# Shifting activation slots and weight tiles within SBUF, without touching an instruction

## The chip, the core and the metric

The kernel runs on one core of a Trainium2 chip. The metric is the device time of one execution in microseconds (us), as the median of several runs. A lower number is better.

## The reference, cut to what matters

The input `x` has shape (4, 1024, 256) in fp32. Three residual layers follow each other. The first and the third are the same gated feed-forward network with ternary weights, the second is a long convolution (a state-space kernel evaluated through an FFT) with a projection.

```python
x = x + 0.5 * ffn(layernorm(x))
x = x + (gelu(causal_conv(layernorm(x), K)) @ W.T + b)
x = x + 0.5 * ffn(layernorm(x))

def ffn(x):                                     # widths 256 -> 1024 -> 1024 -> 1024 -> 256
    h = silu((x @ w1.T) * s1) * ((x @ w2.T) * s2)
    h = gelu((h @ h1.T) * t1)
    h = gelu((h @ h2.T) * t2)
    return (h @ w3.T) * s3
```

Nearly all of the arithmetic is in the two feed-forward layers, and most of that in the two 1024 x 1024 products with `h1` and `h2`.

## The kernel before, in words

The 4096 rows of `x` are cut into 8 blocks of 512 rows (`TB = 512`). Each block goes through the feed-forward network once for the first layer (tiles with `_f` in their names) and once for the third (`_g`), so there are 16 passes of `ffn`. All five weight matrices stay in SBUF for the whole kernel, in the pool `keep`, as the tiles `w1_sb`, `w2_sb` (8 KB per partition each), `h1_sb`, `h2_sb` (32 KB each) and `w3_sb` (8 KB). The profile cuts digits and buffer numbers out of the names, so `w1_sb`, `w2_sb` and `w3_sb` are all `w_sb` there, and `h1_sb` and `h2_sb` are both `h_sb`.

Weights are ternary, so they are exact in the fp32r format. Activations are held as two fp32r parts, a rounded one and the remainder (`parts = 2`), and every product is done twice, once for each part, into the same PSUM bank. A tile of activations is therefore 128 partitions by 2 by 512 numbers, 4096 bytes per partition. These tiles (`xt`, `ha`, `h2`, `h3`) share one set of 15 slots, given out by the helper `ring` (line 134), one slot directly after the other in SBUF. Tiles of 512 numbers (`half`, 2048 bytes) share another set of 19 slots.

The inner work is `linear` (line 235): for every output tile of 128 features it goes over the input tiles `k` and the two parts, and issues one matmul each:

```python
for k in range(n):
    for part in range(parts):
        nc.tensor.matmul(ps, w[:, k, m * P : (m + 1) * P], acts[k][:, part, :], ...)
```

The first operand is the stationary one: a block of 128 columns of a weight tile, 512 bytes per partition. The second is the moving one: 512 numbers of one part, 2048 bytes per partition. In a trace each such call is a LDWEIGHTS (engine row PEld) and a MATMUL (row PE). The LDWEIGHTS of the next call runs while the MATMUL of the present one streams. In the last product (line 295, tiles `po`) the roles are swapped: 128 columns of an activation slot are stationary and 256 columns of `w3_sb` are moving.

One pass of `ffn` issues 64 matmuls into `pa` and `pb` (the products with `w1` and `w2`), 256 into `p` (with `h1` and `h2`) and 64 into `po`. Sixteen passes make 5120 matmuls of 512 moving columns and 1024 of 256 moving columns, all in fp32r. The rest of TensorE's matmuls are in fp32: transposes of the normalised input (`pt`, line 225), the taps of the convolution's kernel (`pk`, line 497), and the transforms and projection of the middle layer (`pf` line 561, `pi` line 731, `pw` line 751).

ScalarE applies the activation out of PSUM (lines 258 and 271) and writes the rounded part (lines 261 and 273). VectorE multiplies by the gate (line 259) and forms the remainder (line 217). The convolution's own work is woven in by generators that are advanced once per output tile. A tile framework inserts the semaphores and orders each engine's instructions.

Where tiles lie: the allocator places each pool's tiles one after another. Before the change `w1_sb` starts at byte 17,408 of each partition, `w2_sb` at 25,600, `h1_sb` at 33,792, `h2_sb` at 66,560 and `w3_sb` at 99,328, and the ring's slots start at 165,376 and then every 4096 bytes (from 169,472, with small tiles in between, once more shifted by a multiple of 512). Every one of these numbers is a multiple of 512, and so is the offset of every column block inside a weight tile and of every part inside a slot.

Of the kernel before, what the change touches and what calls it, by code (L numbers as in the profile page):

```python
# [17 lines left out]
P = 128  # L18
B, L, D = 4, 1024, 256
HID = 1024  # L20
J = L // P
DC = D // P
KH = HID // P
# [68 lines left out]
def macaron_layers(  # L92
# [25 lines left out]
    wide = F32R if split else F32  # L118
    parts = 2 if split else 1
    keep = ctx.enter_context(tc.tile_pool(name="keep", bufs=1))  # L120
    work = ctx.enter_context(tc.tile_pool(name="work", bufs=2))
# [11 lines left out]

    def ring(name, *shape, dtype=F32):

        return work.tile([P, *shape], dtype, tag="ring", name=name, bufs=15)

    sc_sb = keep.tile([P, 4, KH], F32, name="sc_sb")  # L140
    cst_sb = keep.tile([P, CST_WIDTH], F32, name="cst_sb")
    ident = keep.tile([P, P], F32, name="ident")
    make_identity(nc, ident)
    w1_sb = keep.tile([P, DC, HID], wide, name="w1_sb")
    w2_sb = keep.tile([P, DC, HID], wide, name="w2_sb")
    h1_sb = keep.tile([P, KH, HID], wide, name="h1_sb")
    h2_sb = keep.tile([P, KH, HID], wide, name="h2_sb")
    w3_sb = keep.tile([P, KH, D], wide, name="w3_sb")
    wt_sb = keep.tile([P, DC, D], F32, name="wt_sb")
    w3s_sb = keep.tile([P, D], F32, name="w3s_sb")  # L150
    bias_sb = keep.tile([P, D], F32, name="bias_sb")
# [67 lines left out]
    def transposed(xn, name):  # L219

        xt = []
        for k in range(DC):
            pt = bank(f"pt_{name}_{k}")
            for i in range(JT):
                nc.tensor.transpose(  # L225
                    pt[:, i * P : (i + 1) * P], xn[:, i, k * P : (k + 1) * P], ident
                )
            t = ring(f"xt_{name}_{k}", parts, TB, dtype=wide)
            nc.vector.tensor_copy(t[:, 0, :], pt)  # L229
            if split:  # L230
                low_part(t, pt)
            xt.append(t)
        return xt
# [13 lines left out]
    def ffn(xt, src, dst, blk, name, tick, ahead):  # L247
# [4 lines left out]
        for m in range(KH):  # L252
            pa, pb = bank(f"pa_{name}_{m}"), bank(f"pb_{name}_{m}")
            linear(pa, w1_sb, m, xt)
            linear(pb, w2_sb, m, xt)
            g = half(f"g_{name}_{m}")
            t = ring(f"ha_{name}_{m}", parts, TB, dtype=wide)
            nc.scalar.activation(g, pa, AF.Silu, scale=sc_sb[:, 0, m : m + 1])  # L258
            stt(g if split else t[:, 0, :], pb, sc_sb[:, 1, m : m + 1], g, ALU.mult, ALU.mult)  # L259
            if split:  # L260
                nc.scalar.copy(t[:, 0, :], g)  # L261
                low_part(t, g)
            ha.append(t)
        for layer, w in ((2, h1_sb), (3, h2_sb)):
            hb = []
            for m in range(KH):
                ps = bank(f"p{layer}_{name}_{m}")
                linear(ps, w, m, ha)
                t = ring(f"h{layer}_{name}_{m}", parts, TB, dtype=wide)
                g = half(f"g{layer}_{name}_{m}") if split else t[:, 0, :]  # L270
                nc.scalar.activation(g, ps, AF.Gelu, scale=sc_sb[:, layer, m : m + 1])  # L271
                if split:
                    nc.scalar.copy(t[:, 0, :], g)  # L273
                    low_part(t, g)
                hb.append(t)
                if layer == 3:
                    ahead()
                if m < KH - 1:
                    tick()
            ha = hb  # L280
# [558 lines left out]
def macaron_kernel(tc: tile.TileContext, *args):  # L839
    nc = tc.nc  # L840
    with tc.tile_pool(name="flag", bufs=1) as flags:
        bad = flags.tile([1, 1], I32, name="bad")
        macaron_layers(tc, bad, *args)
        n_bad = nc.values_load(bad, min_val=0, max_val=1 << 24)
        with tc.If(n_bad > 0):
            macaron_layers(tc, None, *args)
# [65 lines left out]
```

## Time and profile before

| what | value |
|---|---|
| median of 3 runs | 1465.45 us (1464.86 to 1466.04) |
| the profiled execution, its own time | 1466.05 us |
| its span, first to last instruction | 1464.1 us |
| time outside the span | 1.95 us |
| mean granted TensorE clock | 0.995 |
| TensorE matmul busy | 1429.7 us, 98% |
| VectorE / ScalarE / GpSimd busy | 59% / 45% / 5% |

The span is the time from the first to the last instruction. A matmul's recorded duration contains its latency, which overlaps the next matmul; the pace of a stream is therefore read from how many matmuls start in a stretch of time, not from the duration of one.

### The profile page before, as it was taken

How to read it: one execution, taken by the hardware profiler on the slowest of the kernel's cores; microseconds unless marked ns; L12 is line 12 of the kernel's file. 1: busy time of each engine (PE TensorE's matmuls, PEld its weight loads, DVE VectorE, ACT ScalarE, POOL GpSimd, SP SyncE). 2: the span in 40 equal slices, each digit the busy share in tenths (PEclk: the TensorE clock that was granted, in tenths of full speed). 3: DMA queues.
4: the chain of work that ended last, by engine and by line, in shares of the span. 5: the costliest groups of instructions: out<-in, count | busy, mean ns of one | idle time of the engine just before them, and what ended most of it. 6: DMA issues, size and time to landing. Idle time of an engine off the chain costs nothing.

```text
span 1464.1 us, 18076 instructions
## 1 busy us (share of the span) xinstructions
PE 1429.7 (98%) x7074; PEld 1213.7 (83%) x7074; DVE 860.5 (59%) x1616; ACT 666.1 (45%) x996; POOL 74.4 (5%) x71
## 2 busy tenths in 40 slices
PE   5999999999999999997999999999999999999997
PEld 4788888888888888886888888888888888888886
DVE  5776574765744634667367673676736667464521
ACT  3677353783534434442454344543445334353432
POOL 2000000000000000000100001000010000100000
PEclk9999999999999999999999999999999999999999
DMA  9110000100001111210312113121121111633000
GB/s 365 33 42 2 15 30 4 40 1 29 15 29 44 62 46 38 72 58 29 101 51 87 37 36 94 48 89 37 36 94 44 65 37 36 221 117 101 21 9 17
DMA packets 42975, 85.50 MB, mean 58 GB/s; under 512 B 4737, under 2 KB 9985, under 8 KB 42881
## 3 DMA queue, kind: packets, MB, share of 16 engines
q1 hardware_dynamic: 39088, 72.73, 15.1%
q0 software_dynamic: 3792, 11.54, 2.2%
q8 instruction: 57, 0.93, 0.3%
q14 instruction: 38, 0.30, 0.1%
HBM read 69.05 MB, written 15.20 MB: 58 GB/s over the span
## 4 chain that ended last, share of the span: by engine, by line
PE 94%; DMA 2%; DVE 2%; ACT 1%; issue 0%; POOL 0%; SPq 0%; POOLq 0%; DVEq 0%
PE p_f L239 32%; PE p_g L239 30%; PE po_f L295 4%; PE po_g L295 4%; PE pa_g L239 4%; PE pb_g L239 4%; PE pa_f L239 3%; PE pb_f L239 3%; PE pi L731 2%; PE pf_m L561 2%; PE pk L497 2%; PE pw L751 2%; DMA x_f<-in_x_dram 1%; DMA k_in<-in_kin_dram 1%; PE pt_f L225 1%; DVE given L328 1%
## 5 line engine op out<-in xcount | busy, mean ns | idle before, releaser
L239 PE MATMUL p_f<-ha_f,h_sb 128*128 128x512 f32 x1024 | 242.4, 394 | 1.8 <-ACT ha_f L261 0.9
L239 PE MATMUL p_f<-h_f,h_sb 128*128 128x512 f32 x1024 | 240.4, 392 | 0.0
L239 PE MATMUL p_g<-h_g,h_sb 128*128 128x512 f32 x1024 | 236.0, 390 | 0.0
L239 PE MATMUL p_g<-ha_g,h_sb 128*128 128x512 f32 x1024 | 234.5, 390 | 0.0
L239 PEld LDWEIGHTS p_f<-ha_f,h_sb 128*128 128x128 f32 x1024 | 192.2, 189 | 43.5 <-ACT ha_f L261 1.6
L239 PEld LDWEIGHTS p_g<-ha_g,h_sb 128*128 128x128 f32 x1024 | 192.2, 188 | 39.9
L239 PEld LDWEIGHTS p_g<-h_g,h_sb 128*128 128x128 f32 x1024 | 192.2, 188 | 39.8
L239 PEld LDWEIGHTS p_f<-h_f,h_sb 128*128 128x128 f32 x1024 | 190.9, 188 | 40.0 <-DVE h_f L217 0.3
L271 ACT ACTIVATE g_g<-p_g,sc_sb 128x512 f32<-128x512 f32 x128 | 88.2, 689 | 273.4 <-PE p_g L239 268.6
L217 DVE TENSOR_TENSOR h_f<-g_f,h_f 128x512 fp32r<-128x512 f32 x128 | 88.3, 691 | 193.0 <-ACT h_f L273 192.8
L271 ACT ACTIVATE g_f<-p_f,sc_sb 128x512 f32<-128x512 f32 x128 | 88.0, 688 | 245.6 <-PE p_f L239 245.3
L217 DVE TENSOR_TENSOR h_g<-g_g,h_g 128x512 fp32r<-128x512 f32 x128 | 88.4, 691 | 171.4 <-ACT h_g L273 171.1
L273 ACT CAST h_g<-g_g 128x512 fp32r<-128x512 f32 x128 | 79.4, 620 | 3.9
L273 ACT CAST h_f<-g_f 128x512 fp32r<-128x512 f32 x128 | 79.1, 619 | 3.4
L258 ACT ACTIVATE g_g<-pa_g,sc_sb 128x512 f32<-128x512 f32 x64 | 44.0, 687 | 66.5 <-PE pa_g L239 64.4
L239 PE MATMUL pa_f<-xt_f,w_sb 128*128 128x512 f32 x256 | 70.5, 395 | 1.8 <-DVE xt_f L229 1.2
L259 DVE SCALAR_TENSOR_TENSOR g_g<-pb_g,sc_sb,g_g 128x512 f32<-128x512 f32 x64 | 47.9, 748 | 37.2 <-PE pb_g L239 29.8
L239 PE MATMUL pb_f<-xt_f,w_sb 128*128 128x512 f32 x256 | 69.2, 392 | 0.0
L239 PE MATMUL pa_g<-xt_g,w_sb 128*128 128x512 f32 x256 | 68.6, 390 | 0.0
L239 PE MATMUL pb_g<-xt_g,w_sb 128*128 128x512 f32 x256 | 68.4, 389 | 0.0
L295 PE MATMUL po_g<-w_sb,h_g 128*128 128x256 f32 x512 | 64.2, 285 | 2.2 <-DVE h_g L217 2.2
L295 PEld LDWEIGHTS po_g<-w_sb,h_g 128*128 128x128 f32 x512 | 62.3, 192 | 2.9 <-DVE h_g L217 2.8
(216 smaller groups left out, 1682.3 us busy)
## 6 DMA issues: line engine op xcount, KB each, us to landing
h_sb<-in_h_dram POOLq DMA_DIRECT2D x8, 1024.0 KB, 22.6
given<-in_h_dram SPq DMA_DIRECT2D x32, 256.0 KB, 4.7
kr<-k_hat SPq DMA_DIRECT2D x20, 256.0 KB, 2.7
ki<-k_hat SPq DMA_DIRECT2D x20, 256.0 KB, 2.9
x_f<-in_x_dram SPq DMA_DIRECT2D x8, 512.0 KB, 3.8
xr_f<-in_x_dram SPq DMA_DIRECT2D x16, 256.0 KB, 3.5
x<-y_f SPq DMA_DIRECT2D x16, 256.0 KB, 2.4
xm<-x SPq DMA_DIRECT2D x8, 512.0 KB, 4.1
```

The lines of the kernel that those rows point to most:

```text
L217: tt(t[:, 1, :], src, t[:, 0, :].bitcast(F32), ALU.subtract)
L225: nc.tensor.transpose(pt[:, i * P : (i + 1) * P], xn[:, i, k * P : (k + 1) * P], ident)
L239: nc.tensor.matmul(ps, w[:, k, m * P : (m + 1) * P], acts[k][:, part, :], start=(k == 0 and part == 0), stop=(k == n - 1 and part == parts ...
L258: nc.scalar.activation(g, pa, AF.Silu, scale=sc_sb[:, 0, m : m + 1])
L259: stt(g if split else t[:, 0, :], pb, sc_sb[:, 1, m : m + 1], g, ALU.mult, ALU.mult)
L271: nc.scalar.activation(g, ps, AF.Gelu, scale=sc_sb[:, layer, m : m + 1])
L273: nc.scalar.copy(t[:, 0, :], g)
L295: nc.tensor.matmul(ps[:, e * D : (e + 1) * D], ha[k][:, part, (i + e) * P : (i + e + 1) * P], w3_sb[:, k, :], start=(k == 0 and part == 0) ...
L497: nc.tensor.matmul(pk[:, at + i, :, :].rearrange("p h b -> p (h b)"), a[:, i].rearrange("p a b -> p (a b)"), qd[d1 // per_tile][:, at + i, ...
L561: nc.tensor.matmul(ps[e][:, part, :], m[:, e, part, :], rows_of(q + JQ * e), start=True, stop=True)
L731: nc.tensor.matmul(banks[dc][e][:, q * P : (q + 1) * P], vs[q + JQ * e][:, part, dc * P : (dc + 1) * P], m[:, e, part, :], start=(part == ...
L751: nc.tensor.matmul(ps[:, e * D : (e + 1) * D], yts[dc][j // JQ][:, (j % JQ + e) * P : (j % JQ + e + 1) * P], wt_sb[:, dc, :], start=(dc == 0),
```

## The change

The change moves tiles in SBUF and does nothing else. A ring slot becomes 8 numbers (32 bytes) longer than the tile it holds, so that neighbouring slots start 4128 bytes apart. Each of the five weight tiles gets a gap of 8 to 112 numbers behind it. The tile handed to the rest of the kernel is a view with the same shape as before. The gaps add up to 1024 bytes, so the tiles that follow the weights keep their places modulo 512.

```diff
     def ring(name, *shape, dtype=F32):
-        return work.tile([P, *shape], dtype, tag="ring", name=name, bufs=15)
+        a, b = shape
+        t = work.tile([P, a * b + 8], dtype, tag="ring", name=name, bufs=15)
+        return t[:, 0 : a * b].rearrange("p (a b) -> p a b", a=a)
+
+    def spaced(name, k, width, gap):
+        t = keep.tile([P, k * width + gap], wide, name=name)
+        return t[:, 0 : k * width].rearrange("p (k o) -> p k o", k=k)
...
-    w1_sb = keep.tile([P, DC, HID], wide, name="w1_sb")
-    w2_sb = keep.tile([P, DC, HID], wide, name="w2_sb")
-    h1_sb = keep.tile([P, KH, HID], wide, name="h1_sb")
-    h2_sb = keep.tile([P, KH, HID], wide, name="h2_sb")
-    w3_sb = keep.tile([P, KH, D], wide, name="w3_sb")
+    w1_sb = spaced("w1_sb", DC, HID, 8)
+    w2_sb = spaced("w2_sb", DC, HID, 24)
+    h1_sb = spaced("h1_sb", KH, HID, 112)
+    h2_sb = spaced("h2_sb", KH, HID, 24)
+    w3_sb = spaced("w3_sb", KH, D, 88)
```

In the built program the start addresses become, modulo 512: `w1_sb` 0, `w2_sb` 32, `h1_sb` 128, `h2_sb` 64, `w3_sb` 160, and the 15 slots 0, 32, 64 and so on to 448. The instructions of every engine are the same, in the same order and with the same shapes.

## The prediction

> **What bounds the kernel now.** I read the first part of the page, then the waits of TensorE, then the chain of waits in order of time.
>
> ```profile
> PE 1429.7 (98%) x7074; PEld 1213.7 (83%) x7074; DVE 860.5 (59%) x1616; ACT 666.1 (45%) x996; POOL 74.4 (5%) x71
> PEclk9999999999999999999999999999999999999999
> PE 94%; DMA 2%; DVE 2%; ACT 1%; issue 0%; POOL 0%; SPq 0%; POOLq 0%; DVEq 0%
> ```
>
> TensorE is busy for 98% of the span, its clock is never throttled, and the chain that ended last runs through it for 94%. The waits confirm that nobody holds it up for long; these rows are "who waited, for whom: us in total, times, longest":
>
> ```profile
> PE pt_f L225 <- DVE x_f L211: 13.8, 1, 13.8
> PE pi L731 <- DVE v_False L722: 7.4, 1, 7.4
> PE po_g L295 <- DVE h_g L217: 2.2, 2, 1.3
> ```
>
> One wait at the start, one in the middle layer, and 2 us for the activations. So the end is set by the pace of the matmul stream itself. The chain in order of time gives that pace; its rows are start, length, then what and how many:
>
> ```profile
> 767.59 54.42 PE p_g L239 x240
> 822.88 7.67 PE po_g L295 x64
> 884.87 6.91 PE pw L751 x32
> ...
> 208.38 3.63 PE p_f L239 x16
> 212.01 0.80 PE pk L497 x8
> 212.81 3.78 PE p_f L239 x16
> ```
>
> Dividing: an fp32r matmul of 512 moving columns takes 54.42/240 = 226.75 ns, one of 256 columns 7.67/64 = 119.84 ns. The difference, 106.9 ns for 256 columns, is 0.4176 ns a column, so 512 columns stream in 213.8 ns and **12.9 ns per matmul do not depend on the columns**. The third row is fp32: 6.91/32 = 215.9 ns for 256 columns, at half the rate[...]. So each of the 6144 fp32r matmuls seems to carry some 10 ns that a fp32 one doesn't. All of them have both operands starting at a multiple of 512 bytes, and in the trace the LDWEIGHTS for the next matmul starts 3 or 4 ns after the present matmul.
>
> The last three rows are a second clue. Sixteen matmuls take 3.63 us when the stream is settled (226.9 ns each), but 3.78 us after eight small `pk` matmuls. The single starts after such a break lie 324, 235, 233, 236, 224, 231, 236, 228, 233, 230 and then 227 ns apart: the first is a weight load that nothing covered, and about nine more run slow until the two streams are in step again. The pace thus depends on how the weight stream and the moving stream lie against each other in time. That is what an address could act on.
>
> [...]
>
> **The change part by part.**
>
> *Instructions.* None is added, removed or moved, on any engine or queue; no wait is added. In the before version all 6078 pairs of a streaming fp32r matmul and the next fp32r weight load start at distance 0 modulo 512. Counted from the new addresses, the distances spread over all sixteen multiples of 32, between 277 and 428 pairs each; 397 stay at 0.
>
> *TensorE, the term that decides.* The trace has no fp32r matmul at another distance, so I bound it. The best case removes the whole 10.4 ns: 6144 x 10.4 = 63.9 us. The worst is priced among the rivals. For the value between I use the speeds. The `pk` rows, 0.80/8 = 100 ns each with only 16 columns to stream, are paced by weight loads, so a load walks its 512 bytes in about 100 ns. The moving stream walks 512 bytes (128 columns) in 128 x 0.4176 = 53 ns. During one load it makes about two rounds modulo 512 while the weights make one. Started together they meet at the beginning and once more one round later, at the end; started apart they meet once, in the middle. If a meeting is what costs, **half the excess goes**: 32 us, for 15 in 16 of the pairs: 30.0 us. That is a reading of the clues, not something that the trace shows.
>
> *VectorE and ScalarE* read and write the same slots in the same order. They have 41% and 55% of the span free, and TensorE waits for them 2 us at a time at most once the stream has begun, the middle layer's 7.4 us apart, which touches no ring tile. Their reads and writes already sweep through all places modulo 512. I price them at nothing. What hides them is TensorE's own stream; faster matmuls thin that cover, and `ha` and `h` (lines 261 and 217) would be late first, at layer boundaries. Bounds: 1 us gained, 3 us lost over the 32 layer boundaries and the 16 `po`.
>
> *DMA.* The weights land in rows shifted by multiples of 32 bytes. The first matmul waits for `x_f` (the 13.8 us), and the first stretch of 50 us has 17 us of idle TensorE, in which weight loads of 9.0 and 22.6 us play a part. Bytes and packets are the same, so nothing; bounds plus or minus 1 us.
>
> *Sum.* Against the profiled execution, which took 1466.05 us (span 1464.1 and 1.95 around it): 1466.05 - 30.0 = 1436.0. The median of the runs is 0.6 us lower, 1465.45; against it 1435.5, my forecast.
>
> **The rivals.**
>
> *A fixed cost of fp32r (no change, 1465.4).* The 12.9 ns may be the price of swapping fp32r weights, whatever the addresses. For it: it is 226.75 to the ns in settled stretches, equal for 512 and 256 columns, whatever VectorE and ScalarE do meanwhile[...]. Against it: after a break single distances fall to 224 and rise to 236, which a fixed cost doesn't explain.
>
> *The streams no longer settle (slower, 1479).* Today every operand starts at the same place, so after some nine matmuls the two streams find a step in which 226.75 ns repeat. Of 3.78 - 3.63 = 0.15 us lost after a break about 0.10 us is the uncovered load (324 - 227 ns), and 0.05 us is spread over nine matmuls: 5.5 ns each. With slots 32 bytes apart, the moving operand changes its place in 2491 of 5053 consecutive pairs of 512-column matmuls (the two parts of one slot keep it). If each such change is a new disturbance of 5.5 ns, 13.7 us are lost: 1479. If the stream never settles, all 6144 pay: 33.8 us, 1499. This decides when the disturbance outweighs what the distance gives, by more than 0.5 ns a matmul.
>
> *The full removal (1402).* Only distance 0 and its neighbours cost anything, all others run at 216 ns. For it speaks only that the fp32 rows show such a floor.
>
> *The change doesn't do what it says.* The places of the five weight tiles hardly matter: 15 slots at 15 of 16 places give nearly all distances to any weight tile. That part is near nothing in each case; the slots' spacing carries the change.
>
> **How the numbers follow.** A measurement of this kernel can tell about 0.2%, or 2.9 us, from no change. Faster, from the half gain to the full one and with smaller gains: 0.62. Within 0.2%, the fixed cost: 0.12. Slower, streams that don't settle: 0.26; the slow stretches after a break are the only place where the trace shows another alignment in time, and there it costs. The forecast is 1435.5 us, the likeliest case, whose own range is 1402 to 1460. Since the signs differ, the range for 8 in 10 reaches from the full removal, 1402, past no change and the rival's 1479 with its 3 us of unknown late activations: 1482. Outside lie a stream that never settles and a gain beyond the fp32 floor.
>
> **What would show it.** Right: in the chain in order of time 240 `p_g` matmuls in about 53.2 us instead of 54.42, 64 `po_g` in about 7.35, `pw` unchanged at 6.91 for 32, and TensorE still above 95%. The fixed cost is right if 54.42 stays to the last digit. The second rival is right if the settled rows rise to 55 us or more, and a row like 3.63 no longer differs from one like 3.78 after `pk`. The forecast is wrong in its mechanism if the gain or loss appears in waits for `ha` or `h`, or in the first 50 us.

## The result: slower by 1.4%

The changed kernel takes 1486.37 us (median of 4 runs, 1484.25 to 1488.44) against 1465.65 us. The ratio is 1.0143, 95% interval 1.0128 to 1.0158. The forecast of 1435.5 us had the wrong sign, and the measured time lies 4 us above the end of the range.

These are the rows of the changed kernel's page that answer to those shown of before: busy time by engine, the granted clock, and the shares of the chain that ended last.

```profile
PE 1451.2 (98%) x7074; PEld 1212.0 (82%) x7074; DVE 861.4 (58%) x1616; ACT 667.0 (45%) x996; POOL 74.2 (5%) x71
PEclk9999999999999999998999999999999999999999
PE 95%; DVE 2%; DMA 2%; ACT 1%; issue 0%; SPq 0%; POOL 0%; POOLq 0%; DVEq 0%
```

The span grew from 1464.1 to 1483.3 us, by 19.2, and TensorE's busy time from 1429.7 to 1451.2, by 21.5. The granted clock, which the prediction called never throttled, was 0.50 in the kernel before from 41.1 to 44.6 us (inside the matmul stream), from 689.7 to 696.5 and in the last 3 us, and in the changed one from 694.8 to 705.1 and in the last 3 us. VectorE and ScalarE do the same work in the same time within 1 us. The two largest of TensorE's waits are those of before too (that for `h_g` is 0.5 us instead of 2.2):

```profile
PE pt_f L232 <- DVE x_f L218: 13.8, 1, 13.8
PE pi L738 <- DVE v_False L729: 7.4, 1, 7.4
```

So nothing new is waited for. The matmul stream itself runs at another pace, as the chain of the changed kernel in order of time shows (start, length, what, how many):

```profile
1149.48 55.69 PE p_g L246 x240
1206.04 7.58 PE po_g L302 x64
1268.99 6.91 PE pw L758 x32
...
209.37 3.71 PE p_f L246 x16
213.08 0.80 PE pk L504 x8
213.88 3.80 PE p_f L246 x16
```

An fp32r matmul of 512 columns now takes 55.69/240 = 232.0 ns instead of 226.75. One of 256 columns takes 7.58/64 = 118.4 instead of 119.8, a little less. The fp32 stream `pw` is unchanged to the digit. And the difference between a stretch before and one after a `pk` break, 0.15 us before the change, is 0.09 now. What is left is the late weight load after the break: the load behind the first `p_f` matmul starts 83 ns after it, where the others start 2 or 3 ns after theirs, and the first distance there is 316 ns, 84 more than the 232 of the others. (Before the change it starts 83 ns late too, so "a weight load that nothing covered" was not what the trace shows.) Otherwise the undisturbed stretch has become as slow as the disturbed one.

A recorded duration of `p_g`, 395 ns in the mean (390 of before), reaches past the next start. From the starts in the trace, the 5120 matmuls of 512 columns fill 1207.3 us instead of 1185.0 (22.3 more), the 1024 of 256 columns 124.0 instead of 127.7 (3.7 less), and all else 130.5 instead of 130.1. That sums to 19.0 of the 19.2 us.

### The profile page after: what moved, and what is told of

It reads as the page before. It is cut to its first block, busy times and chain, and to the rows that moved or that the text cites. A ratio compares the mean times of both kernels' runs of the same rounds, so it can differ in the third digit from the quotient of the medians.

```text
span 1483.3 us, 18076 instructions
## 1 busy us (share of the span) xinstructions
PE 1451.2 (98%) x7074; PEld 1212.0 (82%) x7074; DVE 861.4 (58%) x1616; ACT 667.0 (45%) x996; POOL 74.2 (5%) x71
## 4 chain that ended last, share of the span: by engine, by line
PE 95%; DVE 2%; DMA 2%; ACT 1%; issue 0%; SPq 0%; POOL 0%; POOLq 0%; DVEq 0%
PE p_f L246 32%; PE p_g L246 31%; PE po_f L302 4%; PE pb_g L246 4%; PE pa_g L246 4%; PE po_g L302 4%; PE pb_f L246 4%; PE pa_f L246 3%; PE pi L738 2%; PE pw L758 2%; PE pf_m L568 2%; PE pk L504 2%; DMA x_f<-in_x_dram 1%; DMA k_in<-in_kin_dram 1%; PE pt_f L232 1%; DVE given L335 1%
## 5 line engine op out<-in xcount | busy, mean ns | idle before, releaser
L246 PE MATMUL p_f<-h_f,h_sb 128*128 128x512 f32 x1024 | 244.5, 396 | 0.0
L246 PE MATMUL p_g<-h_g,h_sb 128*128 128x512 f32 x1024 | 241.3, 395 | 0.0
L246 PE MATMUL p_g<-ha_g,h_sb 128*128 128x512 f32 x1024 | 239.9, 395 | 0.0
L302 PE MATMUL po_f<-w_sb,h_f 128*128 128x256 f32 x512 | 63.1, 282 | 0.0
```

Source lines behind the costliest of these rows:

```text
L302: nc.tensor.matmul(ps[:, e * D : (e + 1) * D], ha[k][:, part, (i + e) * P : (i + e + 1) * P], w3_sb[:, k, :], start=(k == 0 and part == 0) ...
```

## The experiments

Every kernel below has the instructions of the kernel before, in the same order; only start addresses differ. "Distance" is the place of the stationary operand that is loaded during a matmul, minus the place of that matmul's moving operand, modulo 512 bytes. In the `pa`, `pb` and `p` products the weights are stationary and a slot moves; in `po` it is the other way round.

*Settled* paces in this section are means of the time from one matmul's start to the next, taken over matmuls that follow at least 24 undisturbed ones of the same weight tile; for 512 columns there are some 1280 of `h1` and 1170 of `h2` in each run, for `po` some 550. For `w1` and `w2`, which alternate in short groups, the mean of all is given.

### One half of the change at a time

Slots alone (`slots_only`) and weights alone (`weights_only`). The helper `placed` gives a tile with so many numbers left free ahead of it and behind it, as the change's `spaced` does behind it:

```diff
-        return work.tile([P, *shape], dtype, tag="ring", name=name, bufs=15)
+        a, b = shape                                   # slots_only
+        t = work.tile([P, a * b + 8], dtype, tag="ring", name=name, bufs=15)
+        return t[:, 0 : a * b].rearrange("p (a b) -> p a b", a=a)
...
-    h1_sb = keep.tile([P, KH, HID], wide, name="h1_sb")
+    h1_sb = placed("h1_sb", KH, HID, 24, 0)        # weights_only: gap ahead, gap behind
+    h2_sb = placed("h2_sb", KH, HID, 112, 0)
... (w1_sb, w2_sb and w3_sb likewise)
```

Expected of the slots alone: 

> Only the slots are 4128 bytes apart; the weight tiles stay at multiples of 512. Theory 'loss of step' (a distance between weights and slot that changes from matmul to matmul keeps the weight stream and the moving stream from settling): the same loss as the full change, 1483 to 1489 us, and 240 p_g in about 55.7 us. Rival 'each weight tile's own place counts': clearly better than the full change, near 1475 us or less.

Measured: 1487.46 us, ratio 1.0152 (1.0134 to 1.0171). `h1` settles at 231.98 ns, `h2` at 232.12. The slots alone do all of it, as the prediction's last rival had said of the two halves. A row of its chain:

```profile
1150.55 55.66 PE p_g L241 x240
```

Expected of the weights alone: 

> Only the weight tiles move (places 0, 32, 128, 64, 160 modulo 512); all slots stay at 0, so that within the h1 and the h2 product the distance is not 0 but constant. Theory 'loss of step': the streams settle again, each product to a constant pace, and the time is within 1% of before, 1455 to 1475 us; in the pa/pb stage alone, where weights at 0 and at 32 alternate, some loss, at most 5 us. Rival 'any distance but 0 costs 5 ns a matmul': 1483 us or more, with p_f and p_g at about 232 ns.

Measured: 1488.71 us, ratio 1.0169 (1.0152 to 1.0186). The theory of the "loss of step" falls here, and its rival's 1483 us or more came. With all slots at the same place the distance within one product is constant, and yet the product with `h1` (distance 128) runs at 232.45 ns and that with `h2` (distance 64) at 233.33. The row of the chain within the last `h2` product of this kernel:

```profile
1441.58 27.07 PE p_g L244 x116
```

27.07/116 = 233.4 ns. Its single distances from start to start alternate between 236 and 230 or 231 ns: the streams do settle, but into a pattern whose mean is 233.33 ns. With 6.67 ns called a round, that is 35 rounds; the 226.67 of before are 34. So a constant distance other than 0 can cost as much as a changing one.

### Only multiples of 64 between the slots

`slots_64` pads a slot by 16 numbers instead of 8.

> Slots 4160 bytes apart, so all at multiples of 64, weights at multiples of 512. In the settled stretches of before all starts agree modulo 6.67 ns, the time in which the moving stream reads 64 bytes. Theory 'only the place modulo 64 bytes counts': as before, 1463 to 1468 us. Theory 'loss of step with any changing distance modulo 512': as the full change, 1480 to 1489 us.

Measured: 1482.56 us, ratio 1.0123 (1.0106 to 1.0139); `h1` at 231.44 ns, `h2` at 231.42. The place modulo 64 bytes is not what counts. (6.67 ns for 64 bytes was an estimate: 16 columns at 0.4176 ns, from the rows of before, make 6.68.)

### Constant distances, one by one

In these kernels all slots share one place, and each weight tile has its own; only the gaps differ from the sketch above. One kernel then gives the pace at three or four distances.

`scan_a` (w1, w2 at 96, h1 at 256, h2 at 384): 

> All slots at 0, weights at constant places: w1 and w2 at 96, h1 at 256, h2 at 384, w3 at 224 modulo 512. Theory 'loss of step': each product settles to one constant pace. If the two streams' meeting costs, as the prediction had it, the products with h1 (half a round apart) settle below 226.75 ns, at 216 to 222, and the whole is faster than before, 1430 to 1455 us. If the 12.9 ns are a fixed cost of fp32r once settled: 226.75 again and 1463 to 1468 us.

Measured: 1479.71 us, ratio 1.0107 (1.009 to 1.0124). At 256, half of 512 bytes apart, where the two streams were to meet least, `h1` settles exactly where it was, and `h2` runs in a longer pattern. Neither the forecast of 1430 to 1455 us nor the fixed cost's 1463 to 1468 came. The rows of the chain within the last `h1` and the last `h2` product:

```profile
1403.75 26.29 PE p_g L244 x116
1432.82 26.95 PE p_g L244 x116
```

26.29/116 = 226.6 ns at distance 256, and 26.95/116 = 232.3 at 384. The single distances of starts at 384 repeat the ones at 128 in `weights_only`, number by number: 232, 241, 233, 231, 231, 229, 230, 232, 241 and so on. So 256 acts like 0 and 384 like 128: the pace repeats after 256 bytes.

`scan_b` (w1, w2 at 224, h1 at 192, h2 at 160, w3 at 64): 

> All slots at 0; constant weight places w1 and w2 224, h1 192, h2 160, w3 64 modulo 512. So far distances 0 and 256 settle at 226.7 ns, 64 at 233.3, 128 and 384 wander at 232.4. Theory 'the distance modulo 256 decides, and only 0 is cheap': h1 and h2 both at 230 to 234 ns, 1484 to 1492 us. Rival 'some other distance settles one round of 6.67 ns lower': one of them at 220.0 ns, 14 us less for that product.

Measured: 1485.58 us, ratio 1.0136 (1.012 to 1.0153). `h1` at 230.04, `h2` at 233.33 ns, as the theory of distance 0 modulo 256 had it.

`scan_c` (w1, w2 at 0, h1 at 32, h2 at 224, w3 at 192): 

> All slots at 0; w1 and w2 at 0, h1 at 32, h2 at 224, w3 at 192 modulo 512. Theory 'only distance 0 modulo 256 is cheap': h1 and h2 at 230 to 234 ns, 1482 to 1490 us; the pa/pb stage as before. Rival 'a distance of 32 bytes is still near enough to 0 to settle, or settles lower': h1 or h2 at 226.7 or 220.0 ns, 1475 us or less.

Measured: 1482.55 us, ratio 1.0117 (1.01 to 1.0134). `h1` at 233.29, `h2` at 233.31 ns, as the same theory had it; `po`, at distance 64 modulo 256, settles at 113.64 ns in the mean (113.33 in most passes), far below the 120.0 of before.

`scan_d`: 

> All slots at 0; w1 and w2 at 0, h1 at 16, h2 at 240, w3 at 128 modulo 512. Theory 'only distance 0 modulo 256 is cheap', if what meets are pieces of 32 bytes or more: 16 and 240[...] are still close to 0 and at least one settles at 226.7, 1465 to 1478 us. If the pieces are 16 bytes or less: both at 230 to 234, 1482 to 1490 us.

As built this was another kernel: the tile sizes were rounded up to 32 bytes and moved all slots to 32, so that the distances were 240 (`h1`), 224 (`h2`, `w1`, `w2`) and, for `po`, 144 modulo 256. Measured: 1479.77 us, ratio 1.0096 (1.0079 to 1.0113); `h1` at 227.70 ns, `h2` at 233.32, `po` at 113.34. So 16 bytes short of 0 is nearly as good as 0: some passes of `h1` settle at 226.67 there, the others at 228.33. The expectation for +16 in `h1` was not tried.

`scan_e` and `scan_f` (each timed once) take odd multiples of 16, with gaps that leave every tile a multiple of 32 bytes long, so that the slots stay at 0.

> Distances that are odd multiples of 16: w1 and w2 at 112, h1 at 144, h2 at 176, po at 208 modulo 256, all slots at 0. Theory 'only near 0 is cheap for 512 columns': h1 and h2 between 230 and 234 ns. Rival 'what helps po helps here': h1 at 144 settles at 220.0 ns.

> More odd multiples of 16: w1 and w2 at 208, h1 at 80, h2 at 48, po at 16 modulo 256, all slots at 0. Theory 'only near 0 is cheap for 512 columns': h1 and h2 between 230 and 234 ns. Rival 'another distance settles one round lower': one of them at 220.0 ns.

Measured: 1486.12 and 1489.81 us, without an interval. In `scan_e` `h1` at 233.33 and `h2` at 230.04, in `scan_f` 231.99 and 233.33 ns. No distance of 512 columns settles below 226.67.

All together, by distance modulo 256, in ns:

| distance | 512 columns moving | 256 columns moving (`po`) |
|---|---|---|
| 0 | 226.67 (the same at 256) | 120.4 (120.0 in most) |
| 16 | not tried | 117.5 |
| 32 | 233.3 | 118.7 |
| 48 | 233.3 | |
| 64 | 233.3 | 113.6; 116.0 in `shift64` |
| 80 | 232.0 | |
| 96 | 234.2 (`w1`, `w2`) | 118.0 |
| 112 | 233.3 (`w1`, `w2`) | |
| 128 | 232.5, 232.6 | |
| 144 | 233.3 | 113.3 |
| 160 | 233.3 | |
| 176 | 230.0 | |
| 192 | 230.0, 229.6, 229.3 | 118.0 |
| 208 | 233.1 (`w1`, `w2`) | 118.8 |
| 224 | 233.3, 233.3 | |
| 240 | 227.7 | |

For 512 columns 0 is the cheapest of all; for 256 columns it is the dearest. Where the values at one distance differ, the stream has more than one pattern to settle in. At 192, for 512 columns, a pass runs either at 228.9 or at 233.3 ns; at 64, for `po`, either at 113.3 or at 117.8. The table's means depend on how many passes took which, and what decides that the runs do not show.

### Distance or place?

`shift64` leaves the weights at 0 and moves all slots to 64, by a longer tile ahead of the pools:

```diff
-    bias_sb = keep.tile([P, D], F32, name="bias_sb")
+    bias_sb = keep.tile([P, D + 16], F32, name="bias_sb")[:, 0:D]
```

> Weights at 0, all slots at 64 modulo 512, 4096 bytes apart (a tile ahead of the pools is 64 bytes longer, so the other working tiles move by 64 too). Theory 'the distance decides, not the place': p_f and p_g run as h1 does with weights at 192 and slots at 0, to 0.3 ns. Rival 'an odd place of the moving operand alone costs': differs from that, and near 233.3 ns whatever h1 at 192 does. The fp32 streams pw and pi should keep their pace, 215.9 and 111.6 ns, since both their operands move or they leave slack.

Measured: 1472.74 us, ratio 1.0049 (1.0032 to 1.0066). `h1` and `h2` run at 229.6 and 229.3 ns, within 0.7 ns of `h1` in `scan_b`. That run has the same distance modulo 256 with the weights at 192 and the slots at 0, where here they lie at 0 and 64. The 0.3 ns expected are not met, for the two patterns are mixed differently. The patterns themselves are the same. In the slower one both traces repeat 233, 233, 234 ns, in the faster one 225, 230, 231, 226, 229, 232, 226, 229, 232. The rows of the chain within one product of each, the first two from `scan_b`, the last two from `shift64`:

```profile
1230.87 27.01 PE p_g L244 x118
1414.14 27.07 PE p_g L244 x116
...
1219.47 26.55 PE p_g L239 x116
1398.14 27.07 PE p_g L239 x116
```

That is 228.9 and 233.4 ns in either run. `h2` at distance 224 agrees as well: 233.3 ns with the slots at 0 (`scan_c`) and at 32 (`scan_d`). So the distance decides, not the place of either operand. The fp32 streams kept their pace of 6.91 us for 32 (`pw`) and 7.14 for 64 (`pi`).

### A distance that changes, but only by 256

`h1_256` moves the eight rows of `h1` apart by 256 bytes more:

```diff
-    h1_sb = keep.tile([P, KH, HID], wide, name="h1_sb")
+    h1_sb = keep.tile([P, KH, HID + 64], wide, name="h1_sb")[:, :, 0:HID]
```

> As before, but the eight rows of h1 lie 4352 bytes apart instead of 4096, so in the h1 product the distance changes between 0 and 256 modulo 512 after every input tile. Theory 'only the distance modulo 256 counts': settled at 226.67 ns in h1 as in h2, and the time as before, within 0.2% (1462 to 1469 us). Rival 'every change of distance disturbs the streams': the h1 product at 229 ns or more, 5 us or more in all.

Measured: 1465.23 us against 1464.63, ratio 1.0003 (0.9994 to 1.0011). The length of the row is that of before to the digit:

```profile
1131.74 54.42 PE p_g L239 x240
```

A change of distance by 256 bytes disturbs nothing here: 54.42 us for 240, as before.

### Using it: one product out of place

`w3_112` leaves `w1`, `w2`, `h1`, `h2` and all slots where they were and puts only `w3` at 112, so that `po` gets the distance 144 modulo 256:

```diff
-    w3_sb = keep.tile([P, KH, D], wide, name="w3_sb")
+    w3_sb = placed("w3_sb", KH, D, 28, 100)        # gap ahead, gap behind
```

> As before, but w3 at 112 modulo 512, so that only the po product (256 moving columns, slots stationary) has another distance, 144 modulo 256. In the run with w1, w2, h1 and h2 out of place, po settled at 113.3 ns at this distance against 120.0 at 0. Theory 'each product's pace is set by its own distance': po at 113.3 to 116 ns and all else as before: 1024 x 5 to 7 ns, so 1458 to 1461 us. Rival 'the gain is lost in re-settling between products': 1464 us or more.

Measured: 1461.11 us against 1464.63, ratio 0.9976 (0.9964 to 0.9987). This is faster than both kernels. Its chain in order of time:

```profile
1129.97 54.42 PE p_g L244 x240
1185.26 7.29 PE po_g L300 x64
```

`po` takes 7.29 us instead of 7.67 for 64, and the other products are untouched. All of `po` fills 121.8 us instead of 127.7, 5.9 less. The profiled span is 5.6 us shorter (1458.5), but 1.0 us of that is a shorter first wait (12.8 us instead of 13.8), and the other matmuls took 1.1 us more. The medians differ by 3.5 us, 1.9 to 5.3 by the interval, a little less than the 5 to 7 us expected.

## Why the prediction was wrong

**What bounds the kernel** was right: TensorE's own pace sets the end, nobody waits for anything new, and the change acts through nothing but that pace. VectorE, ScalarE, DMA and the first 50 us at no cost were right too: all but the fp32r matmuls changed by 0.4 us.

**The step that failed** is "half the excess goes". Of the 12.9 ns that didn't depend on the columns it took 10.4 for the cost of two meetings of the streams at distance 0, and it made 0 the worst distance although the trace had no other. These 10.4 ns were the author's estimate and were not shown: the rows of before give 226.75 ns for an fp32r matmul of 512 columns and 215.9 for an fp32 one of 256, which is 10.85 apart (with it the same step would gain 31.2 us instead of 30.0). So the sum gained 30.0 us where the runs show a loss: the fp32r matmuls of the changed kernel take 18.6 us more (22.3 more for 512 columns, 3.7 less for 256). The table shows why: for 512 columns 0 is the best of all distances that were tried, and none falls to 216 ns, the 215.9 of the fp32 row that the prediction took for the bound. The picture of the two streams that make one and two rounds of 512 bytes is refuted by `scan_a`, where half such a round apart changes nothing: what repeats is 256 bytes. One reading of the lines was off as well. The 0.80/8 = 100 ns for a `pk` load are an average over unlike distances: the second of the eight starts 26 ns after the first, and each further start comes 112 ns after the one before. That leaves the moving stream at about two rounds for one of the load, so it isn't what went wrong.

**The rival that came nearest** is the second, the streams that no longer settle. It was right on the sign, on the place (the 512-column products) and on what the profile would show: settled rows went from 54.42 to 55.69 us, and a row after `pk` hardly differs from one without. Its size was wrong in who pays. It charged 5.5 ns to the 2491 matmuls before which the slot changes; the trace shows 22.3 us over 5120, which is 4.4 ns on each. The upper end of 33.8 us was charged also to the 1024 of `po`, which gained.

Its mechanism was right only in small part. `weights_only` and the scans show that a distance needn't change to cost: each constant distance has its own pace, between 226.7 and 234.2 ns. And in the settled stretches of the changed kernel a matmul whose successor reads the same slot takes 231.5 ns, one whose successor reads another slot 232.2 (some 1250 of each). Both lie about 5 ns above the 226.7 of before, so the matmuls that the rival let go free pay nearly as much as the others.

How the distances combine inside the changed kernel is not shown. The simple mean over the eight multiples of 32 in the table (230.0 at 192) is 232.1 ns, and the changed kernel, whose distances spread over them, runs at 232.0. But this may be no more than an agreement of numbers: its matmuls at distance 0 take 231.7 ns, and those of `slots_64` at distance 0 take 232.7. In these two kernels a matmul doesn't get the pace of its own distance (226.7 ns at 0) when its neighbours have others.

**"The weight places hardly matter"** was right inside this change (1487.46 us without them against 1486.37 with them) and wrong in general: alone they cost 1.7%.

**The fixed-cost rival** falls: the part that does not depend on columns moves with addresses. The 12.9 ns belong to distance 0 alone. At distance 144, 512 columns take 233.3 ns and 256 columns 113.3; a line through these two would leave less than nothing for the fixed part. The place of one operand against the other changes the pace by up to 7.5 ns in 227, with no instruction changed. What couples the two streams no run shows.

What stays open is why: which part of the memory or of TensorE makes 256 bytes of distance equal to none, why 512 moving columns like distance 0 and 256 columns dislike it, what picks one of two patterns at the same distance, and what keeps the rounds of 6.67 ns. The runs show the dependence, not its cause.

## What to carry to other kernels

In this kernel, where TensorE is the bound and each fp32r matmul has its own weight load, addresses are part of the pace (226.7 to 234.2 ns for 512 columns), and the alignment that looked like a conflict was the best one for 512 columns. In a kernel like it, measure the pace by distance before spreading tiles. One product was tuned by the place of its own weight tile alone (`w3_112`), and a chain row of a few dozen matmuls shows the gain: 7.67 to 7.29 us for 64 of `po`. A bound worked out from the distance between two rows (226.75 against 215.9 ns) says how much could be there, not that the next edit takes it.

## What was not expected of the hardware

- In the mean over its pattern, an fp32r matmul of 512 columns takes 34 rounds of 6.67 ns (226.67) at distance 0 and 256, and 35 rounds (233.33) at 32, 48, 64, 144, 160 and 224; one of 256 columns takes 18 rounds (120.0) at distance 0 and 17 (113.33) at 144. The paces in between are patterns over several matmuls: the nine of 225 to 232 ns above sum to 2060 ns, which is 309 rounds.
- In all settled stretches of the kernel before, the starts have the same phase modulo 6.67 ns, apart from a slow drift of 2 ns over the whole run, although stretches of fp32 matmuls lie between them. What keeps that phase no run shows.
- The fp32 streams showed no dependence: `pw` took 6.91 us for 32 and `pi`, after its first pass, 7.14 for 64 in the chains of both kernels and of the ten experiments other than `scan_e` and `scan_f`, also with the slots and the working tiles moved by 64 bytes.
